# A two-layer transformer on one core: expert tiles turned by VectorE and DRAM from the ninth on, a 1.5 MB load at another step, a different last stretch of the integer FFN

## The chip, the cores and the metric

The kernel runs on one core of a Trainium2 chip. The metric is the device time of one execution in microseconds (us), the median of three runs. The profile is of one further execution. TensorE is called PE in its lines, VectorE DVE, ScalarE ACT, GpSimd POOL, and SyncE, which issues most DMAs, SP.

## The reference

Eight sequences of 512 tokens with 512 features, all float32, pass two layers. Each half of a layer ends with a layer norm.

```python
x = layernorm(x + attention0(x))   # 16 heads of 32, causal, biases
x = layernorm(x + experts(x))      # 8 experts, top 2 per token, LoRA on router and experts
x = layernorm(x + attention1(x))   # RMS norm, 8 query heads of 64 on 2 key groups, own residual
x = layernorm(x + ffn(x))          # 512 -> 1408 -> 512, integer weights with a scale per row

def experts(x):                    # per token
    p = softmax(router(x)); w, e = top_k(p, 2); w = w / w.sum()
    return sum(w[k] * (silu(gate[e[k]](x)) * up[e[k]](x)) @ down[e[k]] for k in range(2))
```

## The kernel before, in words

**Attention 0** runs over batches b = 0 to 7, head groups g = 0 to 3 (four heads side by side) and three units u of key tiles. `scores` fills one PSUM tile `sc` (one buffer) and ScalarE takes its exp; `product` and `normalise` follow a unit later, `rs` being the sums of a group. Work of the batch before is hung into slots `todo[g, u]`: `project`, the turn of its normed rows, the router's `score`, `choose` (top 2 and running counts, a chain of small VectorE steps with one small exp on ScalarE), `dispatch`, `one_hot` and `enter`, which writes tokens into a table. TensorE's order is the program's order near the end; the other engines are ordered by a scheduler until the expert tiles are past the twelfth, and from there they, and SP, are in program order too.

**Expert tiles.** Tokens are gathered per expert in tiles of 128 rows. There are 48 fixed tiles and then free ones. Tiles 0 to 15 (`n_soon`) are drawn from a table that lacks the last two batches, so that they can start while batch 7 is still in work; tile 16 and later need the full table (`of_fixed`, set after the `enter` of batch 7). `Tiles.step` number i issues the matmuls `half(i + 2)` (gate and up of a pair of tiles, L942 and L957 in the profile), gathers rows to come (`fetch`, a GpSimd indirect DMA), and `down(i)` (L982), whose result y is copied by VectorE for even i and by ScalarE for odd i (L204, L202) and written by SP (L991).

A tile's rows have to be turned (features on partitions) before `half`. There are two ways. `turn_rows` has TensorE transpose four blocks into PSUM (L923), and VectorE or ScalarE copies them out (L924). `blocks` and `pair_back` have VectorE turn 32x32 blocks (L903), SP write a pair of tiles to DRAM (L911, 512 KB), and SP read it back in four DMAs that put the blocks in place (L917, 128 KB each). `BY_BLOCKS` is the first tile that takes the second way. Buffers: six for gathered rows (`xr`), four for turned pairs (`xrT`), two for y, two PSUM banks for `ps_y`, two named `mm` for small products.

**Beside the tiles**, the dictionary `beside` runs pieces at chosen steps: two loads of 1 MB (`load_rows`, L1954, x<-rows) when 18 and 24 steps are done, and from step 36 on the first pieces of attention 1, which scale its weights `w_qkv` (1.5 MB, loaded at L147 when `Attention1` is built, after step 11).

**The integer FFN** (`IntegerFfn`) runs batch by batch over 11 chunks c of 128 hidden units: `hidden` makes `ps_g` and `ps_u` (L1222) and splits the product into a high and a low half on ScalarE and VectorE (L1227, L1232, L1233), and `out` adds a chunk to four token tiles (L1238). In the last batch the outputs of the last `HELD` chunks are held back until all chunks are there; then the token tiles are finished and normed by `last_rows`.

Of the kernel before, what the change touches and what calls it, by code (L numbers as in the profile page):

```python
# [9 lines left out]
F32 = mybir.dt.float32  # L10
# [3 lines left out]
AF = mybir.ActivationFunctionType  # L14
ALU = mybir.AluOpType
# [3 lines left out]
P = 128  # L19
NB = 8  # L20
S = 512
D = 512
NT = S // P
ND = D // P
E = 8
R = 16
NHID = 1408 // P
# [40 lines left out]
def in_order(tc, *engines):  # L68


    return tc.manual_schedule(engines={mybir.EngineType.PE, *engines})
# [755 lines left out]
class Tiles:  # L827
# [4 lines left out]
    NI = 256 // P  # L832


    BY_BLOCKS = 18

    def __init__(self, env, router, w, dram):
        self.env, self.nc, self.router, self.w = env, env.nc, router, w
        self.drams = [dram.tile([P, 4 * ND, 2 * 32], F32, name=f"pair_{i}") for i in range(4)]
        half = range(E // 2), range(E // 2, E)  # L840
        runs = [(range(0, SOON, 2), part) for part in half] + [(range(SOON, FIXED, 2), range(E))]
        self.order = [(j + i, e) for js, part in runs for j in js for e in part for i in range(2)]
        self.n_soon = len(half[0]) * SOON
        self.n = N_FIXED + N_FREE - RARE
        self.xrs, self.xTs, self.hs, self.hTs, self.ats, self.pairs = {}, {}, {}, {}, {}, {}
        self.next = self.n_banks = 0

    def open(self, ctx):
        tc = self.env.tc
# [154 lines left out]

    def open_rows(self):

        for i in range(4, 8):
            self.fetch(i)
        for i in range(2, 4):
            self.turn_rows(i, self.nc.scalar.copy)  # L1010

    def step(self):
        i = self.next
        self.next += 1
        if i == 0:
            self.down(i)
        if i + 2 < N_FIXED:
            self.half(i + 2)
        elif N_FIXED <= i + 1 < self.n:
            self.gate_up(i + 1, lambda: self.turn_hidden(i))  # L1020
        elif i + 1 == self.n:
            self.turn_hidden(i)
        if i + 8 < self.BY_BLOCKS:
            self.fetch(i + 8)
        if i + 10 >= self.BY_BLOCKS:
            self.fetch(i + 10)
        if i:
            self.down(i)
        for n in (4, 5) if i == 0 else (5,):
            if i + n < self.BY_BLOCKS:  # L1030
                self.turn_rows(i + n)
        if i + 6 >= self.BY_BLOCKS:
            self.pair_back(i + 6)
        if i + 7 >= self.BY_BLOCKS:
            self.blocks(i + 7)
# [109 lines left out]
class IntegerFfn:  # L1145

    HELD = 4

    def __init__(self, env, guard, weights, rows, dram):
        self.env, self.nc, self.guard, self.weights, self.rows = env, env.nc, guard, weights, rows
# [95 lines left out]
    def batch(self, b):  # L1248
        env, nc = self.env, self.nc
        os = [self.p_o.tile([P, D], F32, tag=f"o{t}", name=f"ps_f{t}") for t in range(NT)]  # L1250
        final = b == NB - 1
        hold = NHID - self.HELD if final else NHID
        parts = {}
        for c in range(NHID):
            parts[c] = self.hidden(b, c, c >= hold)
            if 0 < c <= hold:
                for t in range(NT):
                    self.out(os, t, c - 1, parts[c - 1])

            if not final and c < NT:  # L1260
                self.blocks(b + 1, c)
            if not final and 0 <= c - 6 < ND:
                self.parts(b + 1, c - 6)
        if not final:
            for t in range(NT):
                self.out(os, t, NHID - 1, parts[NHID - 1])
            for t in range(NT):
                self.scaled(b, os, t)
            env.layernorm(b, lambda t: env.ins.out[b][ts(t, P), :])
            return  # L1270

        order = [(t, c) for ts_ in ((0, 1), (2,), (3,)) for cs in (range(hold, NHID - 1), (NHID - 1,)) for t in ts_ for c in cs]
        for t, c in order:
            self.out(os, t, c, parts[c])
            if c == NHID - 1:
                self.last_rows(b, t, self.scaled(b, os, t))

    def last_rows(self, b, t, x):
        nc, small, env = self.nc, self.env.small, self.env
        stats = small.tile([P, 6], F32, name="stats2")  # L1280
        mv = small.tile([P, 2], F32, name="mv2")
        rstd = small.tile([P, 1], F32, name="rstd2")
        nc.vector.bn_stats(out=stats, in_=x)
        nc.vector.bn_aggr(out=mv, in_=stats)
        nc.gpsimd.tensor_scalar(rstd, mv[:, 1:2], LN_EPS, None, ALU.add)
        nc.gpsimd.tensor_tensor(rstd, rstd, env.neg_half[:, :1], ALU.pow)  # L1286
        shift = small.tile([P, 1], F32, name="shift2")
        nc.gpsimd.tensor_scalar(shift, mv[:, 0:1], rstd, -1.0, ALU.mult, ALU.mult)  # L1288
        nc.scalar.activation(x, x, AF.Identity, bias=shift, scale=rstd)
        nc.scalar.dma_start(out=env.ins.out[b][ts(t, P), :], in_=x)  # L1290


def attention0(env, guard, keep, routes, experts, dram, p_mm, tiles_ctx):
# [4 lines left out]
    tc, nc, ins, xs, vec = env.tc, env.nc, env.ins, env.xs, env.vec  # L1298
# [3 lines left out]
    with ExitStack() as phase:  # L1302
# [56 lines left out]
        def mm(shape, name):  # L1359
            return p_mm.tile(shape, F32, tag="mm", name=name)  # L1360
# [11 lines left out]
        def query(b, g):  # L1372
            ps = mm([P, S], "ps_q")
            for c in range(ND):
                multiply(ps, wq[:, g, ts(c, P)], xts[b][:, c, :], c)
            q = own.tile([P, S], F32, tag="q", name="q", bufs=2)
            if g == ND - 1 and 0 < b <= by_blocks:

                nc.scalar.activation(q, ps, AF.Identity, bias=vec[:, V_BQ + g : V_BQ + g + 1])
            else:  # L1380
                nc.vector.tensor_scalar(q, ps, vec[:, V_BQ + g : V_BQ + g + 1], None, ALU.add)
            heads[b, g] = [q]
# [56 lines left out]
        def choose(b, columns=HD):  # L1439
            router.choose(b, logits.pop(b), mm([P, NT, E], "ps_r"), columns)  # L1440
# [66 lines left out]

        def normalise(b, g, acc):
            total, av = acc
            rs = mm([P, S], "rs")  # L1510
            for j in range(4):
                nc.tensor.matmul(rs[HD * j : HD * (j + 1), :], lhsT=ones, rhs=total[:, j, :], start=True, stop=True)
            r_inv = work.tile([P, S], F32, tag="r_inv", name="r_inv", bufs=2)
            guard.watch_sums(rs, r_inv)
            nc.vector.reciprocal(r_inv, r_inv)
            nc.vector.tensor_tensor(aoTs[b][:, g, :], av, r_inv, ALU.mult)
            guard.watch_inverses(r_inv)
# [3 lines left out]
        def plan(b):  # L1521
# [11 lines left out]
            if b:  # L1533
                places = ((1, 0), (1, 1), (1, 2), (2, 0)) if by_dma else ((1, 0), (1, 0), (1, 1), (1, 1) if last else (1, 2))
                for t, slot in enumerate(places):
                    todo[slot].append(lambda t=t: project(pb, t))
                if by_dma:
                    todo[2, 1].append(lambda: blocks(pb))
                else:
                    for c in range(ND):  # L1540
                        at = todo[2, 1] if last and c >= 2 else (late if last else todo)[2, 0]
                        at.insert(c % 2 if at is todo[2, 1] else len(at), lambda c=c: turn(pb, c))
                todo[(3, 2) if by_dma else (2, 1)].append(lambda: score(pb))
                if not by_dma:
                    todo[2, 2].append(lambda: choose(pb))
            if b == 0:
                todo[1, 0].append(lambda: router.merge_lora(mm([P, ND, E], "ps_wr")))
            if b > 1:
# [72 lines left out]
        b = NB - 1  # L1621
# [28 lines left out]
class Attention1:  # L1650
# [6 lines left out]
    def __init__(self, env, guard, router, rows, own, p_mm, dram):  # L1657
        self.turn = Turn(env, dram, NT, "turned1")
        self.env, self.nc, self.guard, self.router, self.own, self.p_mm = env, env.nc, guard, router, own, p_mm
        self.rows = rows  # L1660

        self.w_qkv = own.tile([P, UPS, 512], F32, name="attn1_qkv")
        env.load_units(self.w_qkv, 0, env.ins.w_attn1[:6])
        self.nss = env.norm_scales()
        self.state = {}

    def mm(self, shape, name):
        return self.p_mm.tile(shape, F32, tag="mm", name=name)
# [4 lines left out]
    def prepare(self, b):  # L1673
# [43 lines left out]
        def query(g):  # L1717
# [3 lines left out]
            for c in range(ND):  # L1721
# [3 lines left out]

        return {"fetch": combine.fetch, "add": combine.add, "sum": combine.sum, "stat": combine.stat, "deviations": combine.deviations, "norm": norm,
                "turn": turn, "blocks": blocks, "key": key, "value": value, "query": query}

    def first_pieces(self):

# [207 lines left out]
def usual_pass(tc, ins, held_out):  # L1938
    nc = tc.nc
    with ExitStack() as ctx:  # L1940
# [4 lines left out]
        with tc.tile_pool(name="a_mm", bufs=2, space=PSUM) as p_mm, ExitStack() as attn1_ctx:  # L1945
            with tc.tile_pool(name="routes", bufs=1, side="right") as routes, \
# [12 lines left out]
                attention = Attention1(env, guard, router, rows, own, p_mm, dram)  # L1959
                beside = {tiles.next + 6 * (b + 1): lambda b=b: load_rows(b) for b in range(2)}  # L1960

                for i, piece in enumerate(attention.first_pieces()):
                    beside[E * NT + 4 + 2 * i] = piece
                with in_order(tc, mybir.EngineType.DVE, mybir.EngineType.Activation, mybir.EngineType.Pool,
# [323 lines left out]
```

## Time and profile before

| | |
|---|---|
| median of 3 runs | 2122.95 us (2122.55 to 2125.76) |
| profiled execution | 2119.8 us, of which the span is 2118.1 us |
| TensorE | 2080.9 us busy, 98% of the span |
| VectorE, ScalarE, GpSimd | 1269.7, 606.6 and 498.2 us busy |
| TensorE turns of tiles' rows (L923) | 72 transposes of 128x128, mean 0.27 us |
| block transposes (L903) | 50, 128x512, median 0.702 us |
| pair writes and reads (L911, L917) | 25 and 100 |

A line of the timeline gives start and duration in us, the engine, the line of kernel.py, the operation, the output and inputs, and how many instructions were merged; what stands in brackets is the idle time before it and what ended that. Float32 matmuls other than transposes appear as two records each. An engine named with a q (SPq, ACTq) is the issue of a DMA, and not its transfer. Matmuls are pipelined, so that one starts before the record of the last one ends.

### The profile page before, as it was taken

The page shows a single profiled execution, that of the slowest core. Times are in us where ns is not written, and L with a number is a line of the kernel's source. Part 1 is how long each engine was busy: PE and PEld are TensorE (multiplying, and loading weights), DVE is VectorE, ACT ScalarE, POOL GpSimd, SP SyncE. Part 2 cuts the span into 40 slices and gives each one's busy share as a digit, 9 for nine tenths or more (in the row PEclk, how much of TensorE's full clock was granted, in tenths as well). Part 3 has the DMA queues.
Part 4 walks back from the last instruction along what each step waited for, and adds up shares of the span by engine and source line. Part 5 has one row for each costly group of instructions (what it writes and reads, how often), then busy time and mean ns, then how long its engine had stood idle before and what let it go on. Part 6 is the DMA issues. An engine that isn't in the chain of part 4 may idle for free. (4 is left out here: it accounts for less than half of the span.)

```text
span 2118.1 us, 35841 instructions
## 1 busy us (share of the span) xinstructions
PE 2080.9 (98%) x15114; PEld 1051.5 (50%) x15114; DVE 1269.7 (60%) x1963; ACT 606.6 (29%) x838; POOL 498.2 (24%) x489
## 2 busy tenths in 40 slices
PE   9999999999999999999999999999999999999997
PEld 2333333333334677774433333333334888888886
DVE  3667676776767633224247898887867644555443
ACT  2333323323323111111133333333332322222222
POOL 2343534434333211232042222223101000000000
PEclk9999999999999999999999999999999999999999
DMA  9020303414222447777561322132102311111000
GB/s 323 22 73 29 101 19 108 144 47 155 82 100 101 134 140 225 231 237 210 155 208 50 100 71 80 50 100 80 41 1 70 100 40 60 60 60 60 21 20 22
DMA packets 170588, 208.16 MB, mean 98 GB/s; under 512 B 61851, under 2 KB 115099, under 8 KB 167347
## 3 DMA queue, kind: packets, MB, share of 16 engines
q1 hardware_dynamic: 159136, 170.10, 25.6%
q0 software_dynamic: 10560, 34.61, 5.5%
q8 instruction: 122, 2.00, 0.4%
q10 hardware_dynamic: 722, 1.07, 0.1%
q14 instruction: 48, 0.39, 0.1%
HBM read 129.96 MB, written 75.78 MB: 97 GB/s over the span
## 5 line engine op out<-in xcount | busy, mean ns | idle before, releaser
L1077 POOL TENSOR_TENSOR g_total<-g_total,r_inv 128x512 f32<-128x512 f32 x64 | 90.1, 1408 | 487.3 <-DVE r_inv L1848 269.9
L1470 ACT ACTIVATE p<-sc 128x2048 f32<-128x2048 f32 (+1 forms) x96 | 153.0, 1593 | 178.9 <-PE sc L65 155.3
L1505 DVE TENSOR_TENSOR p<-p 128x1536 f32<-128x1536 f32 (+2 forms) x96 | 149.9, 1562 | 80.3 <-POOL p L1480 70.2
L1227 DVE SCALAR_TENSOR_TENSOR hT<-ps_u,vec,sg 128x512 f32<-128x512 f32 x88 | 65.6, 746 | 188.9 <-PE ps_u L1222 188.9
L1238 PE MATMUL ps_f<-ffn_w,h_half 128*128 128x512 f32 x672 | 169.8, 393 | 2.6 <-DVE h_half L1233 2.0
L957 PE MATMUL ps_gu<-xrT,experts 128*128 128x256 f32 x736 | 166.7, 380 | 0.0
L957 PEld LDWEIGHTS ps_gu<-xrT,experts 128*128 128x128 f32 x736 | 139.2, 191 | 31.9 <-issue 15.6
L1818 ACT ACTIVATE p<-sc 128x1024 f32<-128x1024 f32 x128 | 124.2, 1022 | 99.3 <-PE sc L65 99.3
L1848 DVE RECIPROCAL r_inv<-r_inv 128x512 f32<-128x512 f32 x32 | 107.1, 3346 | 67.6 <-ACT r_inv L1074 67.6
L1238 PEld LDWEIGHTS ps_f<-ffn_w,h_half 128*128 128x128 f32 x672 | 124.5, 188 | 34.6 <-DVE h_half L1233 7.6
L1222 PE MATMUL ps_g<-x_high,ffn_w 128*128 128x512 f32 x352 | 137.3, 390 | 0.8 <-DVE x L1790 0.8
L1222 PE MATMUL ps_g<-x_low,ffn_w 128*128 128x512 f32 x352 | 137.2, 390 | 0.0
L1222 PE MATMUL ps_u<-x_low,ffn_w 128*128 128x512 f32 x352 | 137.2, 390 | 0.0
L1222 PE MATMUL ps_u<-x_high,ffn_w 128*128 128x512 f32 x352 | 137.1, 389 | 0.0
L65 PE MATMUL sc<-qT,kT 64*64 64x512 f32 x1024 | 124.7, 602 | 1.1 <-ACT qT L1724 0.7
L65 PE MATMUL ps_q<-experts 128*32 128x512 f32 x1024 | 120.8, 601 | 4.8 <-DMA experts<-in_xT 4.4
L1480 POOL TENSOR_SCALAR_AFFINE_SELECT p<-p 128x512 f32<-128x512 f32 x128 | 82.7, 658 | 165.1 <-ACT p L1470 155.5
L65 PE MATMUL ps_v<-experts 128*32 128x512 f32 x1024 | 120.9, 595 | 0.0
L1837 PE MATMUL av<-p,v 128*64 128x512 f32 x512 | 120.9, 594 | 0.0
L65 PE MATMUL ps_o<-attn_out,aoT 128*64 128x512 f32 x512 | 116.4, 598 | 0.8 <-ACT r_inv L1074 0.8
L65 PE MATMUL ps_k<-experts 128*32 128x512 f32 x1024 | 116.3, 595 | 0.0
L65 PE MATMUL ps_q<-hT,attn_qkv 128*64 128x512 f32 (+1 forms) x504 | 116.2, 596 | 0.0
(277 smaller groups left out, 3198.0 us busy)
## 6 DMA issues: line engine op xcount, KB each, us to landing
results<-y SPq DMA_DIRECT2D x68, 256.0 KB, 2.7
turned<-turned SPq DMA_DIRECT2D x56, 256.0 KB, 4.1
pair<-xrT SPq DMA_DIRECT2D x25, 512.0 KB, 2.9
xrT<-pair SPq DMA_DIRECT2D x100, 128.0 KB, 3.8
x<-in_x SPq DMA_DIRECT2D x8, 1024.0 KB, 8.3
rows<-x SPq DMA_DIRECT2D x32, 256.0 KB, 2.4
x<-rows SPq DMA_DIRECT2D x16, 512.0 KB, 11.0
experts<-in_xT SPq DMA_DIRECT2D x7, 1024.0 KB, 8.7
```

The costliest lines, as they stand in the source:

```text
L65: nc.tensor.matmul(out[m], lhsT=lhsT[:, m], rhs=rhs, start=start, stop=stop)
L957: nc.tensor.matmul(ps[:, j, :], lhsT=w, rhs=xT[:, c, :], start=c == 0, stop=c == ND - 1)
L1077: self.nc.gpsimd.tensor_tensor(self.total, self.total, r_inv, ALU.add)
L1222: nc.tensor.matmul(ps, lhsT=w[:, ts(dc, P)], rhs=x[:, dc, :], start=(dc, i) == (0, 0), stop=(dc, i) == (ND - 1, 1))
L1227: nc.vector.scalar_tensor_tensor(hT, u, vec[:, V_SU + c : V_SU + c + 1], sg, ALU.mult, ALU.mult)
L1238: self.nc.tensor.matmul(os[t], lhsT=h[:, ts(t, P)], rhs=self.weights(2 * NHID + c), start=(c, i) == (0, 0), stop=(c, i) == (NHID - 1, 1))
L1470: nc.scalar.activation(p, sc[:, :, :width], AF.Exp, scale=scale)
L1480: nc.gpsimd.affine_select(out=first, in_=first, pattern=[[0, 4], [1, P]], compare_op=ALU.is_ge, fill=0.0, base=0, channel_multiplier=-1)
L1505: nc.vector.tensor_tensor(total[:, :, P * kt :], total[:, :, P * kt :], p[:, :, at : at + w], ALU.add)
L1818: nc.scalar.activation(p, sc, AF.Exp, scale=scale)
L1837: nc.tensor.matmul(st["av"][HD * j : HD * (j + 1), :], lhsT=st["v"][:, kt, HD * j : HD * (j + 1)], rhs=p[:, j, :], start=kt == 0, stop=kt ...
L1848: nc.vector.reciprocal(r_inv, r_inv)
```

## The change

- `BY_BLOCKS` goes from 18 to 8, so tiles 8 to 17 are turned by VectorE and DRAM. `open_rows` gathers tiles 4 to 9 instead of 4 to 7. A counter `fetched` keeps the gathers ten tiles ahead of the step, and lets tile 16 and later wait for `of_fixed`.
- The load of `w_qkv` leaves the constructor of `Attention1` and is issued by SP when 28 steps are done.
- `HELD` goes from 4 to 5. The last four token tiles, which were finished as two, one and one with the chunks in two parts, are finished one after the other, in program order on VectorE, ScalarE and GpSimd too. The last of them is scaled by VectorE instead of GpSimd's shift and ScalarE.
- End of layer 0, batch 7: `choose(6)` moves from slot (2, 2) to (3, 0); the query of group 2 is copied out by ScalarE instead of VectorE; the sums `rs` of the last group go to a buffer of the pool `p_av` instead of `mm`.

```diff
 class Tiles:
-    BY_BLOCKS = 18
+    BY_BLOCKS = 8
...
+        self.fetched, self.of_fixed = self.BY_BLOCKS + 2, None
...
     def open_rows(self):
-        for i in range(4, 8):
+        for i in range(4, self.BY_BLOCKS + 2):
             self.fetch(i)
...
     def step(self):
...
-        if i + 8 < self.BY_BLOCKS:
-            self.fetch(i + 8)
-        if i + 10 >= self.BY_BLOCKS:
-            self.fetch(i + 10)
+        while self.fetched <= i + 10 and (self.fetched < self.n_soon or self.of_fixed is not None):
+            self.fetch(self.fetched)
+            self.fetched += 1
...
 class IntegerFfn:
-    HELD = 4
+    HELD = 5
...
-        order = [(t, c) for ts_ in ((0, 1), (2,), (3,)) for cs in (range(hold, NHID - 1), (NHID - 1,)) for t in ts_ for c in cs]
-        for t, c in order:
-            self.out(os, t, c, parts[c])
-            if c == NHID - 1:
+        with in_order(env.tc, mybir.EngineType.DVE, mybir.EngineType.Activation, mybir.EngineType.Pool):
+            for t in range(NT):
+                for c in range(hold, NHID):
+                    self.out(os, t, c, parts[c])
                 self.last_rows(b, t, self.scaled(b, os, t))
...
     def last_rows(self, b, t, x):
...
-        shift = small.tile([P, 1], F32, name="shift2")
-        nc.gpsimd.tensor_scalar(shift, mv[:, 0:1], rstd, -1.0, ALU.mult, ALU.mult)
-        nc.scalar.activation(x, x, AF.Identity, bias=shift, scale=rstd)
+        if t == NT - 1:
+            nc.vector.tensor_scalar(x, x, mv[:, 0:1], rstd, ALU.subtract, ALU.mult)
+        else:
+            shift = small.tile([P, 1], F32, name="shift2")
+            nc.gpsimd.tensor_scalar(shift, mv[:, 0:1], rstd, -1.0, ALU.mult, ALU.mult)
+            nc.scalar.activation(x, x, AF.Identity, bias=shift, scale=rstd)
...
 def attention0
-            if g == ND - 1 and 0 < b <= by_blocks:
+            if (b, g) == (NB - 1, 2) or g == ND - 1 and 0 < b <= by_blocks:
...
-            rs = mm([P, S], "rs")
+            rs = p_av.tile([P, S], F32, tag="av", name="rs") if (b, g) == (NB - 1, ND - 1) else mm([P, S], "rs")
...
-                    todo[2, 2].append(lambda: choose(pb))
+                    todo[(3, 0) if last else (2, 2)].append(lambda: choose(pb))
...
 class Attention1:
-        env.load_units(self.w_qkv, 0, env.ins.w_attn1[:6])
...
+    def load(self):
+        self.env.load_units(self.w_qkv, 0, self.env.ins.w_attn1[:6])
...
 def usual_pass
+                beside[E * NT - 4] = attention.load
```

## The prediction

> **What bounds the kernel now.** I read the page first, then TensorE's waits, then three places in the timeline: the tile steps, the end of layer 0, the tail.
>
> ```profile
> PE 2080.9 (98%) x15114; PEld 1051.5 (50%) x15114; DVE 1269.7 (60%) x1963; ACT 606.6 (29%) x838; POOL 498.2 (24%) x489
> ```
>
> TensorE is busy for 2080.9 of 2118.1 us. So an edit counts only if it removes TensorE time, removes a TensorE wait, or shortens what follows the last matmul. The waits, with total, count and longest in us:
>
> ```profile
> PE ps_q L65 <- DMA experts<-in_xT: 4.4, 1, 4.4
> PE ps_r L65 <- DVE v L1370: 4.3, 6, 0.7
> PE av L1497 <- POOL p L1480: 2.8, 5, 1.0
> PE sc L65 <- ACT p L1470: 2.5, 1, 2.5
> PE ps_f L1238 <- DVE h_half L1233: 2.0, 7, 0.5
> ```
>
> No row is large: the page has no 20 us to be found. The fourth is a single stall, and the change reaches it. Two stretches of TensorE's timeline (start, duration, operation) show a tile step with a turn on TensorE, and steps without:
>
> ```profile
> 756.55 3.62 PE L957 MATMUL ps_gu<-xrT,experts 128*128 128x256 f32 x16
> 760.01 1.88 PE L982 MATMUL ps_y<-experts,h 128*128 128x512 f32 x4
> 761.73 0.60 PE L923 MATMUL ps_xrT<-ident,xr 128*128 128x128 f32 x4
> 762.16 3.62 PE L957 MATMUL ps_gu<-xrT,experts 128*128 128x256 f32 x16
> ...
> 790.00 3.62 PE L957 MATMUL ps_gu<-xrT,experts 128*128 128x256 f32 x16
> 793.45 1.88 PE L982 MATMUL ps_y<-experts,h 128*128 128x512 f32 x4
> 795.16 3.62 PE L957 MATMUL ps_gu<-xrT,experts 128*128 128x256 f32 x16
> ```
>
> A step is 762.16 - 756.55 = 5.61 us with the turn; without, two steps from 790.00 to 800.34 give 5.17. A turn therefore costs 0.44 us of TensorE, less than its row's 0.60, because matmuls overlap.
>
> **Turning tiles 8 to 17 by VectorE and DRAM.** Ten turns leave TensorE: 10 x 0.44 = 4.4 us. One of them buys nothing: at 738.53 a rank matmul waits 0.28 us for VectorE's running count (L553), which hangs on the routing matmul at 731.34 and not on the turn between. That wait grows by the 0.44 saved. So -4.0 us (bounds -4.4 and, if two more turns meet such waits, -3.0).
>
> VectorE trades ten copies of 682 ns for ten block transposes of 702 ns. The new order puts four of these (rows 8 to 11) behind the copy of tile 6: 2.6 us, in a gap that runs from 717.35 to the next y copy at 721.83. Their gathers go out by 699.57 and land about 4 us later. If a row came late, the y copy behind it would wait, but ps_y has two banks. Rows 16 and 17 need the full table (752.40); half(16) runs at 790.0. Cost 0.
>
> SP gets five writes and twenty reads more. Reads of pair (12,13) stand behind the result of tile 7, whose copy ends at 756.94: four issues (2.65 us) and 3.8 us to landing end near 763.2. Their matmul, at 767.77 before, comes three turns earlier, at 766.5. Pair (14,15) has the same 3 us to spare, and the earlier pairs more. Cost 0 while the DMAs keep to the later stage's landing times.
>
> Here a rule of the Trainium skill speaks against the change. "VectorE: DVE Perf Modes", section "The three transpose paths", says that VectorE turns only 32x32 blocks and that a plain copy which finishes the turn by strides is far slower than the DMA's own transpose; its rules for authors send a 128x128 turn to TensorE. This trace does not bear out a loss: 25 such pairs, their reads landing in a median 3.8 us, feed 790 to 953 with no TensorE wait.
>
> **The 1.5 MB load moved** from 752.5 to behind step 27. It leaves a stage where it delayed nothing (0), and enters one where the DMA engines are 79% busy (stage table, 790 to 831). The nearest rows are the two 1 MB loads x<-rows, in SP's queue:
>
> ```profile
> 842.97 2.70 SPq L917 DMA_DIRECT2D xrT<-pair  x4
> 845.72 1.14 SPq L1954 DMA_DIRECT2D x<-rows  x2
> 847.78 0.33 SPq L991 DMA_DIRECT2D results<-y  x1
> 848.40 0.33 SPq L911 DMA_DIRECT2D pair<-xrT  x1
> 852.89 0.32 SPq L991 DMA_DIRECT2D results<-y  x1
> 856.26 2.83 SPq L917 DMA_DIRECT2D xrT<-pair  x4
> ```
>
> The pair's write took 7.8 us instead of 2.8; its reads began at 856.26 and were in by about 862.1, and the matmul that wants them starts at 862.38: 0.3 us to spare. After the first such load (814.74) it was about 1.7. Half a megabyte more (0.52 MB), at the 265 GB/s that the core moved from 821 to 832, is 2.0 us later: a TensorE stall of 0.3 to 1.7 us. I take +0.9, bounds 0 and +3 (the two loads differ by more than a microsecond already). Scaling of the weights begins at step 36, 41 us later: covered.
>
> **End of layer 0.** choose(6) moves one head group on. Before, ScalarE's queue held its small exp ahead of a softmax exp:
>
> ```profile
> 671.20 0.23 ACT L525 ACTIVATE tmp<-tmp 128x32 f32<-128x32 f32 x1 [2.48 <-DVE tmp L524]
> 671.34 1.86 ACT L1470 ACTIVATE p<-sc 128x2048 f32<-128x2048 f32 x1
> ```
>
> The small one waits for VectorE, which is in L1505 until 670.84; the large one's scores were complete at about 670.2; and TensorE waits for it until 673.25, since sc has one buffer. In the new order the large exp is first. The scores then start near 668.8 (ps_r no longer ahead, k ready at 668.72), the exp at 670.0 (1.2 us later, as at 650.93 to 652.15), and TensorE goes on at 671.95: -1.3 us. choose(6) ends 0.75 us later on VectorE, at 676.65; the next sum waits for POOL until 676.8 (678.06 less 1.3), so nothing is late. Bounds -1.6 and 0. The query to ScalarE: it idles 10.19 us there, 0. The sums rs to p_av: that buffer was read out by 684.6, rs runs at 688.29, and the mm bank cost no wait before: 0.
>
> **Tail.** One chunk more is held and each tile ends alone, so the matmul count is unchanged. The first tile now meets chunk 10 after 8 matmuls (before, 12), the pattern of the seven other batches, which wait 2.0/7 = 0.3 us. After the last matmul:
>
> ```profile
> 2109.24 0.37 DVE L1284 BATCH_NORM_AGGREGATE mv<-stats 128x2 f32<-128x6 f32 x2
> 2111.03 1.71 ACT L1289 ACTIVATE x<-x,shift,rstd 128x512 f32<-128x512 f32 x2 [0.94 <-POOL shift L1288]
> 2111.98 1.71 ACTq L1290 DMA_DIRECT2D out<-x  x2
> ```
>
> Before, tiles 2 and 3 share VectorE, POOL and ScalarE, and the last scaling ends at 2112.74. After: matmuls end at 2106.3; y 0.66, x 0.66, stats 0.69, mv 0.18 and gaps: 2108.6; POOL's add 0.22 and pow 0.58 with gaps: 2109.65; VectorE's scaling 0.48 (L195: 1.92 for four): 2110.2. The shift and ScalarE's 0.81 are gone. -2.5 us, bounds -3.0 and -1.5.
>
> **Sum.** -4.0 + 0.9 - 1.3 - 2.5 = -6.9 us. The profiled execution took 2119.8 us (span 2118.1 and 1.7 around it), so 2112.9; the median of the runs stands 3.15 us above it, so **2116.0 us**, 0.33% faster. A change of this kernel can be told from none at about 0.2%, 4.2 us; the three runs lie 3.2 us apart.
>
> **Rivals.**
> - *The moved load costs more than the tail gives.* If it drains before anything behind it, as 9.0 us at 752.5, and the stall lasts for two pairs at 2.5 us each, 5.0 replaces 0.9: 2120.1, no change that can be told. For: 0.3 us to spare. Against: the next pair was on time again at 864.67. Chance 0.07.
> - *TensorE's saved time is returned.* If the early tiles are held by the routing chain of batch 7 (VectorE, L523 to L602) rather than by TensorE, only tail, choice and load remain: -2.9, 2120.0. Against: rows of that stretch show waits of 0.76 and 0.28 us only. Chance 0.06.
> - *Turned rows come late: slower.* The reads wait in SP's queue behind results and writes. If they land in 11.0 us (the median of x<-rows) rather than 3.8, the 3 us to spare become a lack of 4.2 for each of five pairs: +21 against -6.9, 2137. It turns the sign from about 4.4 us per read beyond 3.8 (five pairs late by 1.4). For: the stage also carries gathers and y. Against: the 1.5 MB load has left it, and 790 to 953 runs clean. Chance 0.12, which takes in what the skill's rule would do here.
> - *The small steps fail to pay*: choice 0, tail -1.5, turns -3.0 and load +0.9 give -3.6: 2119.4. Chance 0.04.
>
> The forecast keeps 0.71, and faster by over 0.2% is that alone; the first, second and fourth rival are no change, 0.17; the third is slower, 0.12. The range takes all gains at their good bounds without a stall (-9.0, 2114, less 2 us for the spread of runs) up to the two middle rivals with 1.4 us of spread: 2112 to 2121.5.
>
> **What would show it.** Right: 40 transposes fewer at L923; steps 6 to 12 at 5.17 us; the 2.5 us row of sc on ACT p near 1.2; last out DMA about 4 us after the last matmul; one TensorE wait on xrT near step 32. Wrong: TensorE waits on xrT<-pair before tile 18, several of them after step 27, or VectorE idle on POOL's gathers between 717 and 760.

## The result, and the profile after

The changed kernel takes 2115.49 us (median of 7 runs, 2114.23 to 2120.53). The kernel before took 2124.3 us in the 7 runs beside it, and the ratio is 0.9967 with a 95% interval of 0.9958 to 0.9976. By this ratio that is 7.0 us less (the two medians lie 8.8 us apart). A second comparison gave 0.9977 (0.9967 to 0.9988), 4.8 us less. The forecast was 6.9 us less and 2116.0 us.

The two profiled executions lie at opposite ends of their runs: before's 2119.8 us is below all seven runs, after's 2120.53 us is the slowest of its seven. The spans (2118.1 and 2118.7 us) can therefore not be compared, and I compare stage by stage. For that, each TensorE group's start in one trace is put against the start of the same group in the other.

The page's line of engines after the change has 40 matmuls fewer and 2.6 us less TensorE time; VectorE has 0.9 us more.

```profile
PE 2078.3 (98%) x15074; PEld 1046.9 (49%) x15074; DVE 1270.6 (60%) x1963; ACT 607.0 (29%) x838; POOL 497.6 (23%) x488
```

Those of TensorE's waits after the change that matter here (total, count, longest in us):

```profile
PE av L1500 <- POOL p L1483: 4.3, 5, 1.4
PE ps_gu L958 <- DMA xrT<-pair: 3.2, 1, 3.2
PE sc L65 <- issue: 1.4, 1, 1.4
PE rs L1850 <- DVE total L1831: 1.4, 1, 1.4
PE sc L65 <- ACT p L1473: 1.2, 1, 1.2
PE ps_rank L65 <- DVE earlier L553: 0.7, 1, 0.7
PE rs L1515 <- ACT first_turned L925: 0.6, 1, 0.6
```

The 2.5 us stall of sc on ScalarE's p has become 1.2, as forecast. The wait on the rank matmul is 0.7, the 0.28 plus the 0.44 of one turn. New is the single wait of 3.2 us for a pair of turned tiles. The rows av, sc <- issue and rs L1850 are waits that the change does not touch. They vary between runs: the groups of the earlier batches already start 2.0 us later than before's at 507 us, and those of layer 1 lose a further 2.4 us near 1090. This is where the two profiled executions drift apart.

**Turns.** TensorE's timeline (start and duration in us, then the operation) shows the early steps without a turn:

```profile
754.51 3.62 PE L958 MATMUL ps_gu<-xrT,experts 128*128 128x256 f32 x16
757.97 1.88 PE L983 MATMUL ps_y<-experts,h 128*128 128x512 f32 x4
759.68 3.62 PE L958 MATMUL ps_gu<-xrT,experts 128*128 128x256 f32 x16
```

759.68 - 754.51 = 5.17 us, where it was 5.61. From 678 to 785 us the start of the same group moves from 0.40 us earlier than before to 4.24 us earlier: -3.84 us for ten turns.

**The moved load.** SyncE's queue after the change (start and duration of the issue):

```profile
860.92 2.60 SPq L918 DMA_DIRECT2D xrT<-pair  x4
863.57 0.63 SPq L147 DMA_DIRECT2D attn_qkv<-in_w_attn  x1
864.29 0.49 SPq L992 DMA_DIRECT2D results<-y  x1
864.84 0.41 SPq L912 DMA_DIRECT2D pair<-xrT  x1
869.33 0.32 SPq L992 DMA_DIRECT2D results<-y  x1
876.02 2.61 SPq L918 DMA_DIRECT2D xrT<-pair  x4
```

The write of the pair goes out at 864.84, 1.3 us behind the load, and the read-back that waits for it can only be issued at 876.02: 11.2 us, where the forecast had 7.8 + 2.0 = 9.8. TensorE then waits for the read:

```profile
882.17 5.38 PE L958 MATMUL ps_gu<-xrT,experts 128*128 128x256 f32 x16 [3.19 <-DMA xrT<-pair]
```

Besides the 3.19 us in the bracket, the 16 matmuls behind it take 5.38 us and not 3.62. In this execution the load costs 3.2 + 1.8 = 5.0 us at that place; the aligned starts say 5.1 (from -4.24 to +0.87).

**Tail.** The last matmuls, the issue of the last outputs on ScalarE's queue, and VectorE's scaling:

```profile
2102.48 7.31 PE L1238 MATMUL ps_f<-ffn_w,h_late 128*128 128x512 f32 x31 [0.23 <-DVE h_late L1233]
2112.30 1.99 ACTq L1293 DMA_DIRECT2D out<-x  x2
2113.37 0.55 DVE L1288 TENSOR_SCALAR x<-x,mv,rstd 128x512 f32<-128x512 f32 x1 [1.06 <-POOL rstd L1286]
```

The matmuls end at 2109.79 and the last scaling at 2113.92, 4.13 us later. From the last matmul to the end of the span it was 12.12 us and is now 8.93: -3.2 us. The new order also makes the last matmul end later. From the same group near 2074 us to the end of the last matmul it takes 32.43 us, where before takes 31.89: 0.5 us, of which the bracket shows 0.23.

### The profile page after: what moved, and what is told of

It is laid out like the page before. It is cut to its first block, busy times and chain, and to the rows that moved or that the text cites. A ratio compares the mean times of both kernels' runs of the same rounds, so it can differ in the third digit from the quotient of the medians.

```text
span 2118.7 us, 35798 instructions
## 1 busy us (share of the span) xinstructions
PE 2078.3 (98%) x15074; PEld 1046.9 (49%) x15074; DVE 1270.6 (60%) x1963; ACT 607.0 (29%) x838; POOL 497.6 (23%) x488
```

## The experiments

Ratios are against the kernel before, run on the same chip beside each experiment, with 95% intervals. The first four rows ran on one chip, the next four on a second and the last three on a third, where the kernel before had medians of 2121.38, 2120.01 and 2123.99 us; medians can be compared within such a group alone. The line numbers of a kernel made from before are a little lower than those of one made from after.

| kernel | median, us | ratio |
|---|---|---|
| load back in the constructor | 2119.36 | 0.9992 (0.9983 to 1.0001) |
| load moved only | 2124.33 | 1.0013 (1.0003 to 1.0022) |
| choice moved only | 2119.15 | 0.9987 (0.9976 to 0.9997) |
| tail only | 2118.87 | 0.9992 (0.9983 to 1.0001) |
| turns only | 2123.11 | 1.0010 (1.0001 to 1.0019) |
| changed kernel again | 2115.81 | 0.9977 (0.9967 to 0.9988) |
| load in six parts | 2114.08 | 0.9974 (0.9961 to 0.9986) |
| gap filled | 2121.15 | 1.0003 (0.9994 to 1.0012) |
| all loads in parts | 2116.54 | 0.9963 (0.9949 to 0.9977) |
| query and sums back | 2116.7 | 0.9966 (0.9952 to 0.9979) |
| last tile by ScalarE | 2116.35 | 0.9964 (0.9951 to 0.9978) |

### The load at its old place, the rest changed

```diff
 class Attention1:
+        env.load_units(self.w_qkv, 0, env.ins.w_attn1[:6])
 def usual_pass
-                beside[E * NT - 4] = attention.load
```

> The changed kernel with the 1.5 MB load of w_qkv at its old place (when Attention1 is built). Theory A (the moved load is the price): TensorE's 3.2 us wait on xrT<-pair near 882 us goes, and with it the halved clock of 3.4 us that stands right behind it in the profile (about 1.7 us): 3 to 5 us less than the changed kernel where that wait is as long as in its profile, about 2110 to 2113 us. Rival B (the old place is worse, now that ten more tiles come by DRAM): the load sits in SP's queue between the write of pair (14,15) and the reads of pair (12,13), those land late, TensorE waits 2 us or more near 765, and the time is no lower than the changed kernel's 2115.5.

Measured: 2119.36 us, only 0.08% under before (1.7 us, with an interval that takes in 0), where the full change has 0.33%. By the ratios the move is worth 5.3 us against the first comparison of the full change and 3.1 against the second. SyncE's queue and TensorE's timeline of this kernel show why:

```profile
750.80 0.70 SPq L147 DMA_DIRECT2D attn_qkv<-in_w_attn  x1
755.18 0.33 SPq L992 DMA_DIRECT2D results<-y  x1
755.61 6.36 SPq L918 DMA_DIRECT2D xrT<-pair  x4
```

```profile
768.63 5.38 PE L958 MATMUL ps_gu<-xrT,experts 128*128 128x256 f32 x16 [3.80 <-DMA xrT<-pair]
```

With tiles 8 to 17 going through DRAM, there are now reads of pairs behind the load at its old place. Their four issues take 6.36 us instead of 2.6, TensorE waits 3.80 us and then runs 16 matmuls in 5.38 us instead of 3.62: 5.6 us. Undoing the move does not give the load's cost back; it moves the same kind of stall to the early tiles.

### The load moved, nothing else

```diff
 class Attention1:
-        env.load_units(self.w_qkv, 0, env.ins.w_attn1[:6])
+    def load(self):
+        self.env.load_units(self.w_qkv, 0, self.env.ins.w_attn1[:6])
 def usual_pass
+                beside[E * NT - 4] = attention.load
```

> The kernel before with nothing but the load moved behind step 27. Theory A: one TensorE wait of 1 to 3 us on xrT<-pair near 886 us, a stretch of halved clock behind it if it reaches about 2.5 us; 2 to 5 us slower than before. Rival B: the pair pipeline has slack enough and the wait of the changed kernel came from another part; within 1 us of before.

Measured: +0.13% (0.03 to 0.22), or +2.8 us (0.6 to 4.7). The trace has a wait of 2.04 us at 888.21 for a pair, and the 16 matmuls behind it take 3.69 us, the usual length. About 3 us more are lost at 1088 to 1092, in the part that the edit does not touch. On its own the move makes the kernel slower: the old place delayed nothing as long as tiles before the 18th did not use DRAM.

### The turns alone, load at its old place

```diff
-    BY_BLOCKS = 18
+    BY_BLOCKS = 8
```

(with `open_rows`, `fetched` and `step` as in the changed kernel)

> The kernel before with tiles 8 to 17 turned by VectorE and DRAM, the 1.5 MB load at its old place. By the forecast's terms alone: -4.0 us. Theory A, after the run with the load put back (which showed a TensorE wait of 3.8 us near 765 us and a halved clock behind it, 5.5 us together): the load at its old place takes all of the gain, -4.0 + 5.5 = +1.5 us, between no change and 2 us slower. Rival: the wait there was a chance of that one profile, and the time is 3 to 4 us below before.

Measured: +0.10% (0.01 to 0.19), slower by 2.1 us, although 40 matmuls are gone. TensorE's timeline has the whole reason in one line:

```profile
770.40 6.69 PE L958 MATMUL ps_gu<-xrT,experts 128*128 128x256 f32 x16 [4.16 <-DMA xrT<-pair]
```

The wait of 4.16 us and the 6.69 - 3.62 = 3.07 us by which the matmuls behind it are longer make 7.2 us. The turns still bring their 0.44 us at each step around it. -3.84 + 7.2 is +3.4 us in this execution, inside the interval of the runs (+0.2 to +4.0).

So each half of the change loses alone, +2.8 and +2.1 us by the ratios. With the choice (-2.8) and the tail (-1.7) the four single edits add up to +0.4 us, each known to about 2 us either way; together they give -7.0 and -4.8. The 5 to 7 us between belong to the load and the turns being made together: the turns make the old place dear, and the move takes them out of its way.

### The changed kernel again

> The changed kernel again, beside the others on one chip. Theory A: 0.25 to 0.4% below before; its wait on xrT<-pair varies from one execution to the next (3.2 us in the first profile, which was 5 us above the median of its runs).

Measured: 0.9977. Two waits for pairs came this time: 0.23 us for an early pair (at 765.64) and 1.54 us behind the load (at 881.38), and the matmuls behind were not slower. The cost of the load is thus not a constant: by the aligned starts 1.7 us in this execution, 5.1 us in the first. Layer 1 lost 3.6 us by the aligned starts (rs <- DVE total alone 2.3 us, with a halved clock behind it), which took back what the load had saved.

### The load in six parts

```diff
-    def load(self):
-        self.env.load_units(self.w_qkv, 0, self.env.ins.w_attn1[:6])
+    def load(self, u):
+        self.env.load_units(self.w_qkv, u, self.env.ins.w_attn1[u : u + 1])
...
-                beside[E * NT - 4] = attention.load
+                for u, at in enumerate((14, 16, 20, 22, 26, 28)):
+                    beside[at] = lambda u=u: attention.load(u)
```

> The changed kernel with the load of w_qkv in six parts of 256 KB, behind steps 13, 15, 19, 21, 25 and 27. Theory A (the load's size in one piece makes the pair late, since it queues ahead of the pair's write): each part delays a pair by 1 us at most, TensorE never waits for xrT<-pair, no halved stretch there; 3 to 5 us below the profile of the changed kernel and 0 to 4 us below its median. Rival (bytes count, not the piece: the DMA engines are 79% busy in this stage): several waits of about 0.5 us between 790 and 890, no gain.

Measured: no wait for a pair behind any of the six parts, and every group of matmuls at its usual length. One pair came 0.28 us late at 827.96, behind the first 1 MB load (its last read landed at 827.87). The kernel has the shortest profiled span of all, 2112.5 us. The median, 2114.08 us, is 1.7 us below that of the changed kernel on the same chip, but the two intervals overlap by most of their width: it is not shown to be faster. What its one profile does show is that the stall comes from 1.5 MB standing in one piece ahead of a write that a read depends on, and not from the bytes that the tile stage as a whole has to move. Behind each part the reads of a pair follow its write after 4.8 to 5.6 us, the time of writes with no load ahead (4.9 us in before at 838.07, 5.6 in the changed kernel at 855.36).

### All loads in parts

```diff
-                beside = {tiles.next + 6 * (b + 1): lambda b=b: load_rows(b) for b in range(2)}
+                beside = {18 + 2 * i: lambda i=i: load_rows(i // 2, (2 * (i % 2),)) for i in range(4)}
...
+                for u, at in enumerate((14, 16, 26, 28, 30, 32)):
+                    beside[at] = lambda u=u: attention.load(u)
```

> The changed kernel with w_qkv in six parts of 256 KB (behind steps 13, 15, 25, 27, 29, 31) and the two 1 MB loads x<-rows in four parts of 512 KB (behind steps 17, 19, 21, 23). Theory A (any large load in the tile stage makes a pair late, x<-rows too, with 0.3 us to spare in the first profile and a wait in later ones): no TensorE wait on xrT<-pair in any profile, less spread from run to run, 1 to 2 us below the changed kernel: 0.3 to 0.4% below before. Rival: x<-rows is covered, nothing gained over the spread of w_qkv alone (0.26% below before).

Measured: 0.9963 (0.9949 to 0.9977), no wait for a pair at all, and no gain over the changed kernel's 0.9967 that could be told. In layer 1 its profile has a wait of 2.8 us (sc <- ACT qT) that the previous kernel's lacks. Whether an earlier end of the tiles brings this wait about, or whether it comes and goes by itself, the runs do not settle.

### The choice alone

```diff
-                    todo[2, 2].append(lambda: choose(pb))
+                    todo[(3, 0) if last else (2, 2)].append(lambda: choose(pb))
```

> The kernel before with choose(6) one head group later, nothing else. Theory A: the wait of sc on ACT p at the end of layer 0 falls from 2.5 to 1.2 us, and the 3.4 us of halved clock behind it vanish because they follow a TensorE gap of about 2.5 us: -1.3 and -1.5, together about 2.8 us less than before. Rival C (the halved clock comes at some moment of its own, not by the gap): -1.3 us, and a halved stretch stays somewhere in the layer.

Measured: -0.13% (-0.24 to -0.03), or -2.8 us. By the aligned starts it is 2.5 us, from +2.00 ahead of the place to -0.46 behind it. The wait fell from 2.48 to about 1.2 us, which is the 1.3 us of the forecast. Before's timeline shows the wait and the scores behind it:

```profile
673.25 2.01 PE L65 MATMUL sc<-q,k 32*64 32x384 f32 x32 [2.48 <-ACT p L1470]
```

The rest is in the clock. The two tables by stage below are of the kernel before, then of the changed kernel at the load (columns: the stretch and its length, busy time of TensorE, its weight loads, VectorE, ScalarE and GpSimd with counts, then the granted clock, the DMA share and GB/s):

```profile
669.66:673.07 3.41, 1.11 (x24) 0.16 (x8) 2.84 (x11) 1.87 (x2) 0.10 (x1) 1.00 0.94 374
673.07:676.48 3.41, 3.23 (x40) 1.08 (x40) 2.52 (x17) 1.16 (x2) 0.66 (x1) 0.50 0.10 43
```

```profile
879.69:883.10 3.41, 0.93 (x4) 0.87 (x5) 0.00 (x0) 0.00 (x0) 0.21 (x1) 1.00 0.94 312
883.10:886.51 3.41, 3.41 (x9) 2.66 (x8) 0.00 (x0) 0.00 (x0) 0.00 (x0) 0.50 0.54 183
```

In both, the stall leaves TensorE busy for about 1 of 3.41 us, and in the next 3.41 us the granted clock is 0.50. In the kernel with only the choice moved there is no such stretch. So the forecast priced the wait and missed that the wait also slowed the work behind it.

### The gap filled

If it is the gap that halves the clock, then work of no use in that gap must keep it full. This kernel is the one before with four more matmuls at that point (their product is not used):

```diff
+        def fill():
+            ps = mm([P, S], "ps_fill")
+            for _ in range(4):
+                nc.tensor.matmul(ps, lhsT=wo[:, 0, :P], rhs=wo[:, 0, :], start=True, stop=True)
...
+                if last:
+                    todo[3, 0].append(fill)
```

> The kernel before with four extra float32 matmuls of 128x512 (1.7 us, their result is read by nobody) in the 2.5 us in which TensorE waits for the exp at the end of layer 0. The scores that wait for it start no earlier. Theory A (the halved clock follows the TensorE gap): the gap shrinks to about 0.8 us, no halved stretch follows, the 32 records of sc take 1.1 us and not 2.0: about 1.5 us below before, although there is more work. Rival C (the halved stretch has another cause): it stays at its place, and the time is that of before.

Measured: 1.0003 (0.9994 to 1.0012), no change. TensorE's timeline, and the stage that was halved before:

```profile
671.47 3.70 PE L1566 MATMUL ps_fill<-experts 128*128 128x512 f32 x8
675.67 1.12 PE L65 MATMUL sc<-q,k 32*64 32x384 f32 x32
```

```profile
674.69:678.10 3.41, 3.41 (x54) 1.29 (x53) 2.29 (x16) 1.12 (x1) 0.58 (x1) 1.00 0.05 22
```

The filler took 3.70 us, more than the 1.7 that were expected and more than the gap, so the scores started about 1.2 us later. But the clock stayed at 1.00 and they took 1.12 us, where before they took 2.01. This kernel was 1.2 us behind before's at 421 us, 2.4 us at the scores, and 0.9 and 1.3 us at the two groups behind the next product: the delay was made up. Filling the gap is worth nothing in the end; it shows that the halved clock follows the gap, and that the groups behind run at full speed without it. Further on in this execution two pairs came 1.15 and 1.40 us late (at 833.92 and 866.58). They stand behind the two 1 MB loads, which no experiment but one changes: the reads followed the pairs' writes after 9.1 and 8.3 us, where before's profile has 6.7 and 7.9 and no wait.

### Query and sums back, load in six parts

```diff
-            if (b, g) == (NB - 1, 2) or g == ND - 1 and 0 < b <= by_blocks:
+            if g == ND - 1 and 0 < b <= by_blocks:
...
-            rs = p_av.tile([P, S], F32, tag="av", name="rs") if (b, g) == (NB - 1, ND - 1) else mm([P, S], "rs")
+            rs = mm([P, S], "rs")
```

> The changed kernel with w_qkv in six parts (behind steps 13, 15, 19, 21, 25, 27), and the query of group 2 and the sums of the last group where they were before (VectorE, mm). Forecast: both are covered, 0.0 us; TensorE's waits between 640 and 700 us are those of the changed kernel. Rival: they hold the next bank or VectorE, and a wait of 0.5 us or more comes up there.

Measured: 0.9966 (0.9952 to 0.9979), beside 0.9963 for the kernel with all loads in parts on the same chip. (The six parts stand where the kernel with the load in six parts has them; that one ran on another chip.) The waits between 640 and 700 us are those of the changed kernel (sc <- p 1.2, rs <- first_turned 0.6), and from 670 to 678 us the aligned starts gain 2.46 us in both. Both small moves are worth 0 within what can be measured.

### The tail alone

```diff
-    HELD = 4
+    HELD = 5
```

(with the order of the last tiles and `last_rows` as in the changed kernel)

> The kernel before with five chunks held, each of the last token tiles finished alone and the last one scaled by VectorE. Forecast: 0.3 us of TensorE wait added, the last output DMA issued 2.5 us earlier: about 2.5 us less than before. Rival: the transfers and the end of the program set the time, so that an earlier issue gains under 1 us.

Measured: 0.9992 (0.9983 to 1.0001), -1.7 us with an interval that reaches 0. By the trace, the end of the span comes 9.07 us after the last matmul instead of 12.12. The five profiles with the old tail have 11.59 to 12.12 us (median 11.69), the seven with the new one and VectorE's scaling 8.93 to 9.07 (median 8.96): 2.7 us. Of that, 0.5 us go back, since the last matmul ends that much later in every kernel with the new order: 2.2 us are left, where 2.5 were forecast. The ratio alone would not have shown the gain; the traces do.

### The last tile scaled by ScalarE

```diff
     def last_rows(self, b, t, x):
-        if t == NT - 1:
-            nc.vector.tensor_scalar(x, x, mv[:, 0:1], rstd, ALU.subtract, ALU.mult)
-        else:
-            shift = small.tile([P, 1], F32, name="shift2")
-            nc.gpsimd.tensor_scalar(shift, mv[:, 0:1], rstd, -1.0, ALU.mult, ALU.mult)
-            nc.scalar.activation(x, x, AF.Identity, bias=shift, scale=rstd)
+        shift = small.tile([P, 1], F32, name="shift2")
+        nc.gpsimd.tensor_scalar(shift, mv[:, 0:1], rstd, -1.0, ALU.mult, ALU.mult)
+        nc.scalar.activation(x, x, AF.Identity, bias=shift, scale=rstd)
```

> The changed kernel with its last token tile scaled as the others are (GpSimd's shift, then ScalarE) and not by VectorE. Forecast by the rows: shift 0.27 and scaling 0.81 with their gaps in place of VectorE's 0.55, 0.6 to 0.7 us more between the last mv and the issue of the last output; the other 2 us of the tail's gain stay, since they come from finishing each tile alone. Rival: VectorE's scaling is the main part of the gain, over 1.5 us lost.

Measured: the last output's DMA is issued 4.80 us after the last matmul instead of 4.16, and the span ends 9.77 us after it instead of 8.93. VectorE's scaling is thus 0.64 to 0.84 us of the tail's 2.7; the rest comes from the other parts of the tail's edit (five chunks held, tiles finished singly, three engines in program order), which no run takes apart. The ratio, 0.9964 (0.9951 to 0.9978), cannot tell so little.

This kernel gave one more reading by chance. Its wait for a pair was 2.56 us, longer than before's 2.48, and yet the matmuls behind it took 3.69 us. Its table by stage:

```profile
879.47:882.88 3.41, 1.56 (x7) 1.44 (x8) 0.00 (x0) 0.00 (x0) 0.21 (x1) 1.00 1.05 330
882.88:886.29 3.41, 3.41 (x14) 2.46 (x14) 0.00 (x0) 0.60 (x1) 0.00 (x0) 1.00 0.64 180
```

The wait lay across two windows, TensorE was busy for 1.56 us of the first, and the clock stayed full.

## Why the prediction was right, point by point

- *The time.* 2116.0 us was forecast, 2115.49 measured, and both comparisons lie in the range. The sum came out because two mis-sized terms have opposite signs, so that it hit the first comparison to 0.1 us is luck. By the traces the terms are turns -3.8, choice -2.5, tail -2.2 to -2.7 and load +1.7 to +5.1, together -7.3 to -3.4; measured were -7.0 and -4.8.
- *Turns, forecast -4.0: -3.84.* The step of 5.17 us, the one turn lost to the rank matmul (0.28 to 0.7) and the cover for VectorE's four block transposes all came as worked out. With the load out of the way, the only TensorE wait for an early pair in the profiles of the changed kernel is one of 0.23 us, in the second of them. The 3 us to spare for pair (12,13) were not there, though. The new `fetched` holds the gathers of later rows until the full table is there, and then eight go out in a row, from 751.65 to 760.40 in that profile, where before has three by 760. Three of the pair's four reads have a landing on record there and in the kernel with the load in six parts: they took 7.2 to 8.0 us and not 3.8, and in the latter kernel they were in at 764.78 for a matmul at 765.26. The gathers are the likely reason, since the DMA share from 755 to 765 us is 1.08 in that kernel; no run takes them apart from the reads. So this pair cost next to nothing by a narrow margin, and not by the 3 us that were worked out. The rule of the Trainium skill that the prediction weighed ("VectorE: DVE Perf Modes", section "The three transpose paths") warns of plain copies that turn by strides, where the innermost destination stride is large. The read-back moves contiguous runs of 64 numbers (`f` in `pair_back`), so no run here tests that case; the kernel with the load in six parts has no wait for an early pair at all.
- *Load, forecast +0.9: mis-sized.* Half a megabyte more at 265 GB/s was to make the pair's write take 9.8 us. Four profiles have the load in one piece at this place. Their times in us, first from the issue of the write to that of its reads, then from there to the start of the matmul:

  | profile of | write to its reads | reads to the matmul | TensorE waits | matmuls behind longer by |
  |---|---|---|---|---|
  | changed kernel | 11.2 | 6.2 | 3.2 | 1.8 |
  | changed kernel again | 9.3 | 6.4 | 1.5 | 0 |
  | last tile by ScalarE | 10.1 | 6.6 | 2.6 | 0 |
  | load moved only | 10.4 | 5.8 | 2.0 | 0 |

  What was sized too small is the stall made from this write. The write itself was 1.4 us short in the first profile and 0.4 on average. But the forecast had a stall of 0.3 to 1.7 us and took about the middle, whose lower end goes by the slack behind the first 1 MB load; all four waits lie well above the middle, and three of them above the upper end. The reads were slower too: those at 856.26 in before were in by 861.64, after 5.4 us. (The forecast put that at about 862.1, so before's slack was 0.7 us and not 0.3.) The bound of +3 nearly held for the wait alone and was wrong for the load, since a halved clock of 1.8 us can stand behind it. "It leaves a stage where it delayed nothing (0)" holds for before only: the kernel with the load put back shows 5.6 us there.
- *Choice, forecast -1.3: mis-sized.* The wait fell as worked out, 2.48 to 1.19 us. The halved clock behind it was not in the sum: it gave another 1.5 us, of which a wait on first_turned that grew by 0.3 us took a little back (-1.3 - 1.5 + 0.3 = -2.5).
- *Query and sums, forecast 0: 0*, by the kernel with both put back.
- *Tail, forecast -2.5: -2.2* by the medians of the profiles with either tail (-2.7 and 0.5 back), -2.7 against before's profile alone. The last matmul ends 0.5 us later against a forecast of 0.3, and the last DMA is issued 4.16 us after it (forecast: about 4).
- *Rivals.* The one on the moved load priced it at 5.0 us by two late pairs; one execution did pay 5.1, but by one late pair and the clock, and the medians do not follow it. Turned rows late, the rival on the other side, does happen where the load stays: one pair late by 4.2 us in the kernel with the turns alone, not five. Its reads landed there after 8.5 to 10.9 us, close to the 11.0 of that rival. TensorE's saved time was not returned, and the small steps did not fail.
- *Open.* The waits in layer 1 near 1090 us (0.4 us in before's profile, up to 2.9 in others, with a halved clock behind the longest) and the drift before 507 us lie in parts that no edit touches. The runs of one kernel spread by 2 to 9 us, and part of that may be theirs. No experiment tried their cause.

## What to carry to other kernels

Price a bulk load by what is queued behind it and depends on it: 1.5 MB cost nothing at a place where no read-back followed, and 5.6 us at the same place as soon as one did; in six parts it cost no wait at all. The 1 MB loads cost nothing in before's profile and made two pairs late in another, so a load that is covered in one trace can have under 1 us to spare. When a change moves work into DMAs, look for the large transfers in its new way, and for transfers that it holds back and then lets go in a row. Where another edit moves a large transfer aside, test the two together, since here each alone was a loss. Count a TensorE stall of 2 to 4 us with the clock behind it, which was nothing to 3.1 us more here, and see where it falls before trusting the bracket alone.

## What the runs showed of the hardware

The clock is granted in windows of 3.41 us. The 13 profiled executions have 12 stretches at 0.50 between the first and the last matmul, once the clock had gone full, and every one began a whole number of 3.413 us after that moment: after 195 windows in before, 223 in the kernel with the load put back, 256 in after. What goes with it is TensorE's busy time within such a window. Added up from the matmul records, the windows just ahead of those 12 stretches hold 0.01 to 1.31 us of work, and no other window between that moment and the last matmul holds less than 1.56 us. One of the 12 stretches, at 769.65 in the kernel with the turns alone, lasts for two windows. Its first window, itself at 0.50, holds 2.66 us of work, while the windows at 0.50 after which the clock went back to full hold 3.23 to 3.41. So the limit of 1.31 to 1.56 us is one for windows at full clock; in a window at half clock more was not enough, and this is a single case. A wait of 2.48 us inside one window halved the clock, and one of 2.56 us across two did not.

The Trainium skill, "TensorE: Matmul & The Clock Gate", section "Why this matters for your kernels", advises against idle gaps of over about 3 us, since one idle window returns the clock to half. The runs agree that the clock falls to half, and that it does so by windows. They differ on the gap: 2.48 us was enough here, and the window ahead of a drop was not idle but held up to 1.31 us of work.
